# Routing of two expert mixtures in a twelve-block network on one core: choice by maxima, inversion on four column groups

## The chip, the cores and the metric

The kernel runs on one core of one Trainium2 chip. The metric is device time in microseconds (us) for one execution. Before the change the median of three runs is 3125.39 us (3124.48 to 3126.11).

The engines are named as the profile names them: PE is TensorE (matmuls), PEld its weight loads, DVE is VectorE, ACT is ScalarE, POOL is GpSimd, SP is SyncE, which only issues DMAs. Each engine works through its own list of instructions in order. A DMA issued by POOL or ACT stands in that engine's list like any other instruction.

## The reference

The network takes a latent array `x` of 16 sequences of 64 tokens with 256 channels (1024 tokens) and a context of 16 sequences of 1024 rows with 192 channels. Twelve blocks are applied one after the other, each as `x = x + block(layernorm(x))`: four times cross attention, a mixer (two Mamba kinds, a convolution, a second attention) and a feed-forward mixture of eight experts. The change touches the second and the last mixture. Cut to what they compute:

```python
# L1_ffn: every token goes to its two best experts
probs = softmax(xt @ gate_w.T)
top_w, top_i = top_k(probs, 2)
top_w = top_w / (top_w.sum(-1, keepdims=True) + 1e-9)
h = gelu(einsum('td,ndh->tnh', xt, w1) + b1)            # 256 -> 1024
out_all = einsum('tnh,nhd->tnd', h, w2) + b2            # 1024 -> 256
out = (take(out_all, top_i) * top_w[:, :, None]).sum(1)

# L3_ffn: the same with relu and no 1e-9, and each expert takes at most 256 choices;
# all first choices are counted before all second choices, in order of tokens
pos = place of the choice among those of its expert
valid = pos < 256
gate = topv * valid
out = sum over both choices of gate * (relu(xt @ w1[e] + b1[e]) @ w2[e] + b2[e])
```

`top_k` takes the lower index first where two values are equal. All is float32.

## The kernel before

The 1024 tokens lie as eight tiles of 128 partitions, `X[128, 8, 256]`. Each block normalizes `X` into `xn` (`layernorm`, L208) and transposes that into `xnT` (`norm_T`, L244), channels on partitions. A block's weights come through the pool `w` of five buffers, filled by DMAs on POOL's list (L169), which therefore also loads the weights of later blocks.

**The two mixtures** (`ffn1` L2438, `ffn3` L2553) don't compute all experts for all tokens. They sort the 2048 choices (J = 16 columns of 128: eight tiles for the first choice, eight for the second) into slots, gather the rows of `xn` for 128 slots at a time by an indirect DMA from a copy in DRAM, run them through one expert, scale them, and scatter them by an indirect DMA into a DRAM array `d_y` with one row for a choice. At the end `add_sent` (L2371) adds both rows of each token to `X`. ffn1 has 23 groups of 128 slots; a group belongs to one expert, found at run time, and its weights are gathered too (`up`, `down`, 1 MB each, three buffers). ffn3 has 16 groups, two for each expert, with weights loaded by plain DMAs.

What stands ahead of the loop over groups is done once in a block:

- `gate_logits` (L2151): 16 matmuls into `pgate`, copied to `s`. `softmax8` (L2159) with the exponential on ACT.
- `ranks` (L2178): each of the eight values of a token is compared with all eight, ties by index, so that the number of better ones is its rank `r`. These are passes over 8 x 64 elements.
- `choices` (L2245): `oh` marks expert and choice; a scan and two accumulating matmuls (`pq`) count, for each choice, those before it at the same expert.
- In ffn1 one more matmul (`pn`) gives the totals, from which `base` (where an expert's groups begin) and `whose` (which weight rows a group needs) follow.
- `slots` (L2268): for each choice its slot `sl`, the group as the one-hot row `at`, the lane in the group as the one-hot `inb[128, 16, 128]`. Multiplied by token number and by gate weight, `at` gives `val`. The inversion is 16 accumulating matmuls with `inb[:, j]` as the loaded weights and `val[:, j]` (46 or 32 columns) as the moving operand, into `pi`: for each lane and group the token and the weight. A few small DVE steps make `src` (row to gather), `to` (row to scatter) and `weight`.
- `add_down_bias` (L2190): transposes of the combine weights (`pc`), one copy (`combT`, nine rows with a row of ones), eight matmuls with nine rows each against the biases `downb` (`pb`), and eight additions to `X`.
- `take` (L2320) and `expert` (L2332): token gather, transposes (`pxg`), copy (`xT`), then for each of eight 128-wide hidden pieces the `pu` matmuls and an activation, then the `pd` matmuls and the scaling.

**What sets the order.** A scheduler at compile time places each instruction on its engine's list as soon as its inputs are ready in its own estimate, earlier program text first. Where `set_order(True)` is in force, instructions issued through `self.mm`, `self.tr` or a `Queue` (L183) are chained in the order of the program text for that engine (`in_order`, L172). Before the change neither mixture uses it. PSUM is shared out by `moe_pools` (L2234): two tiles of two banks (`big`) and four of one bank (`mid`).

Of the kernel before, what the change touches and what calls it, by code (L numbers as in the profile page):

```python
# [15 lines left out]
P = 128  # L16
# [62 lines left out]
class Net:  # L79
    def __init__(self, ctx, tc, a):  # L80
# [17 lines left out]
        self.downb = self.const.tile([9, 3, D], F32, name="downb")  # L98
        nc.scalar.dma_start(out=self.downb, in_=a["downb"])
# [12 lines left out]
    def make_masks(self):  # L112
# [27 lines left out]
        nc.gpsimd.iota(self.token, [[P, 2 * NT]], base=1, channel_multiplier=1, allow_small_or_imprecise_dtypes=True)  # L140

# [2048 lines left out]
    def add_down_bias(self, comb, i, big, mid, pool, more=None):  # L2190
# [8 lines left out]
        for t in range(NT):  # L2199
            tok = slice(t * P, (t + 1) * P)  # L2200
            ps = mid.tile([P, 512], F32, tag="m", name="pb")
            self.mm(ps[:, :D], cT[:, tok], self.downb[:, i, :], True, more is None)
            if more is not None:
                more(ps[:, :D], tok)
            nc.vector.tensor_tensor(self.X[:, t, :], self.X[:, t, :], ps[:, :D], ALU.add)
# [39 lines left out]
    def choices(self, r, one, mid):  # L2245
# [4 lines left out]
        oh = one.tile([P, 8, J], F32, name="oh")  # L2250
        upto = one.tile([P, 8, J], F32, name="upto")
        prev = one.tile([P, 8, J], F32, name="prev")
        on = one.tile([P, 8, J], F32, name="on")
        nc.gpsimd.memset(on, 1.0)
        nc.gpsimd.memset(on[:, :, 0], 0.0)
        for k in range(2):
            nc.vector.tensor_scalar(
                oh[:, :, k * NT : (k + 1) * NT], r.rearrange("p t e -> p e t"), float(k), None, ALU.is_equal
            )
        flat = [t.rearrange("p e j -> p (e j)") for t in (upto, on, oh)]  # L2260
        nc.vector.tensor_tensor_scan(flat[0], flat[1], flat[2], 0.0, ALU.mult, ALU.add)
        nc.vector.tensor_tensor(prev, upto, oh, ALU.subtract)
# [3 lines left out]
        return oh, pq[:, :P].rearrange("p (e j) -> p e j", e=8), upto  # L2266

    def slots(self, place, oh, s, one, mid, NG, keep):  # L2268
# [7 lines left out]
        sl, gate, low, t1, t2 = (one.tile([P, J], F32, name=f"sl{i}") for i in range(5))  # L2276
        tmp = one.tile([P, 8, J], F32, name="tmp")
        by_j = tmp.rearrange("p e j -> p j e")
        lane = one.tile([P, P], F32, name="lane")
        nc.gpsimd.iota(lane, [[1, P]], base=0, channel_multiplier=0, allow_small_or_imprecise_dtypes=True)  # L2280
        nc.vector.tensor_tensor(tmp, place, oh, ALU.mult)
        nc.vector.tensor_reduce(sl, by_j, AX.X, ALU.add)
        if keep:
            nc.vector.tensor_reduce(t1, oh.rearrange("p e j -> p j e"), AX.X, ALU.add)
            nc.vector.tensor_scalar(t1, t1, 1.0, -65536.0, ALU.subtract, ALU.mult)
            nc.vector.tensor_tensor(sl, sl, t1, ALU.add)

        at = one.tile([P, J, NG + 1], F32, name="at")
        inb = one.tile([P, J, P], F32, name="inb")
        val = one.tile([P, J, 2, NG], F32, name="val")  # L2290
        nc.vector.tensor_tensor(at, bc(sl, 2, NG + 1), bc(self.nth[:, : NG + 1], 1, J), ALU.is_ge)
        nc.vector.tensor_reduce(low, at[:, :, 1:], AX.X, ALU.add)
        nc.vector.scalar_tensor_tensor(low, low, -float(P), sl, ALU.mult, ALU.add)
        for h in range(4):
            js = slice(h * J // 4, (h + 1) * J // 4)
            nc.vector.tensor_tensor(inb[:, js], bc(low[:, js], 2, P), bc(lane, 1, J // 4), ALU.is_equal)
        nc.vector.tensor_tensor(at[:, :, :NG], at[:, :, :NG], at[:, :, 1:], ALU.subtract)
        nc.vector.tensor_tensor(val[:, :, 0], at[:, :, :NG], bc(self.token, 2, NG), ALU.mult)
        prod = one.tile([P, 8, J], F32, name="prod")
        for k in range(2):  # L2300
            ks = slice(k * NT, (k + 1) * NT)
            nc.vector.tensor_tensor(prod[:, :, ks], oh[:, :, ks], s.rearrange("p t e -> p e t"), ALU.mult)
        nc.vector.tensor_reduce(gate, prod.rearrange("p e j -> p j e"), AX.X, ALU.add)
        nc.vector.tensor_tensor(val[:, :, 1], at[:, :, :NG], bc(gate, 2, NG), ALU.mult)
        pi = mid.tile([P, 512], F32, tag="m", name="pi")
        for j in range(J):
            self.mm(pi[:, : 2 * NG], inb[:, j], val[:, j], j == 0, j == J - 1)

        row, weight, none, second = (one.tile([P, NG], F32, name=f"row{i}") for i in range(4))
        src, to = (one.tile([P, NG], I32, name=f"at{i}") for i in range(2))  # L2310
        nc.vector.tensor_scalar(row, pi[:, :NG], -1.0, None, ALU.add)
        nc.vector.tensor_scalar(second, row, float(N), -float(N), ALU.is_ge, ALU.mult)
        nc.vector.tensor_tensor(second, second, row, ALU.add)
        nc.vector.tensor_scalar(src, second, 0.0, None, ALU.max)
        nc.vector.tensor_copy(weight, pi[:, NG : 2 * NG])
        nc.vector.tensor_scalar(none, row, 0.0, 65536.0, ALU.is_lt, ALU.mult)
        nc.vector.tensor_tensor(to, row, none, ALU.add)
        return src, to, weight

    def take(self, src, g, n, d_x, pool):  # L2320

        xg = pool.tile([P, n, D], F32, tag="xg", name="xg", bufs=3)
        for i in range(n):
            self.nc.gpsimd.indirect_dma_start(
# [113 lines left out]
    def ffn1(self):  # L2438
# [6 lines left out]
        with ExitStack() as es:  # L2445
            one, two, big, mid = self.moe_pools(es, L)
            d_x, d_y = self.rows_dram(es, L)
# [281 lines left out]
```

## Time and profile before

| what | value |
|---|---|
| median of the runs | 3125.39 us |
| the profiled execution's own time | 3139.76 us |
| its span, first to last instruction | 3138.1 us |
| PE busy | 2942.0 us (94%) |
| DVE busy | 1966.8 us (63%) |
| ACT busy | 1340.0 us (43%) |
| POOL busy | 712.7 us (23%) |
| mean granted PE clock | 0.952 |
| ffn1: last gate matmul ends, first `pu` matmul starts | 1393.5, 1426.52 us |
| ffn1: loop over groups | to about 1612 us |
| ffn3: last gate matmul ends, first `pu` matmul starts | 2968.8, 3001.80 us |

How to read it: times inside the profile are counted from the start of the span of one profiled execution, which took 14 us longer than the median of the unprofiled runs. Lines L188 and L191 are the helpers `mm` and `tr`, and L72 is the helper `Queue`, so that operations are told apart by their tiles. In the lists of instructions a row has its start, its length, engine, line, operation, `output<-inputs`, shapes, a count, and in brackets the idle time of the engine before it with what ended that. A float32 matmul appears as two records. The granted clock of PE is 1.00 at full speed and 0.50 at half. The chain of waits is followed back from the last instruction, each step to what released it.

### The profile page before, as it was taken

The numbers are of one execution on the slowest core, as the hardware profiler recorded it, in microseconds if no ns is written. First come the engines' busy times: TensorE is split into PE (matmuls) and PEld (weight loads), VectorE is DVE, ScalarE is ACT, GpSimd is POOL, SyncE is SP. The second block draws the span as 40 slices with busy tenths as digits, with TensorE's granted clock in tenths as the row PEclk, the third lists the DMA queues.
The fourth block names the chain that finished last, engine by engine and source line by source line (L and its number), as shares of the span: only waits on it lengthen the run. The fifth ranks groups of instructions, "written<-read, shape, count | busy, mean of one in ns | idle before, by whom it ended". The sixth has DMA issues, their size and how long they took to land.

```text
span 3138.1 us, 64791 instructions
## 1 busy us (share of the span) xinstructions
PE 2942.0 (94%) x27232; PEld 1792.9 (57%) x27232; DVE 1966.8 (63%) x4085; ACT 1340.0 (43%) x3013; POOL 712.7 (23%) x780
## 2 busy tenths in 40 slices
PE   8999999898999999979978999997999899998797
PEld 4666666565555554458854555544655454546676
DVE  6888886523766656961127777768874667775511
ACT  3555554412554441003325444449851255554211
POOL 1000002400210001014410100026761454541131
PEclk9999999999999999968989999998999999999789
DMA  2001000014223313017751222201111111110233
GB/s 75 32 32 32 22 29 12 18 34 109 63 79 93 99 45 82 21 55 270 296 180 52 72 72 77 65 13 44 41 57 34 60 67 55 70 44 15 95 111 120
DMA packets 73796, 223.05 MB, mean 71 GB/s; under 512 B 17457, under 2 KB 28580, under 8 KB 66594
## 3 DMA queue, kind: packets, MB, share of 16 engines
q1 hardware_dynamic: 45936, 113.99, 11.9%
q0 software_dynamic: 21840, 99.39, 9.4%
q10 hardware_dynamic: 5730, 5.53, 0.6%
q8 instruction: 215, 3.52, 0.5%
q14 instruction: 75, 0.61, 0.1%
HBM read 210.00 MB, written 12.66 MB: 71 GB/s over the span
## 4 chain that ended last, share of the span: by engine, by line
PE 81%; DVE 7%; issue 5%; POOL 2%; ACT 2%; DMA 2%; SPq 0%; POOLq 0%; ACTq 0%; DVEq 0%
PE pss L188 15%; PE o L188 13%; PE psp L188 5%; PE pu L188 5%; PE pkv L188 5%; PE pd L188 5%; PE py L188 4%; PE pst L191 4%; PE psc L188 3%; PE po L188 2%; PE pb L191 2%; PE psq L188 2%; PE psi L188 1%; PE psy L188 1%; PE pg L188 1%
## 5 line engine op out<-in xcount | busy, mean ns | idle before, releaser
L188 PE MATMUL pss<-cT,qw 128*32 128x256 f32 x8192 | 367.7, 385 | 18.8 <-ACT pr L72 18.6
L72 DVE TENSOR_REDUCE nm<-pss 128x2 f32<-128x512 f32 (+1 forms) x384 | 309.5, 862 | 83.9 <-PE pss L188 83.9
L188 PE MATMUL o<-pT,cx 128*64 128x512 f32 (+3 forms) x1088 | 351.7, 576 | 0.0
L72 ACT ACTIVATE pr<-pss,nmm 128x256 f32<-128x256 f32 x512 | 234.8, 485 | 162.2 <-DVE nmm L72 162.2
L188 PEld LDWEIGHTS pss<-cT,qw 128*32 128x32 f32 x8192 | 203.2, 109 | 148.6 <-ACT pr L72 26.3
L188 PEld LDWEIGHTS o<-pT,cx 128*64 128x64 f32 (+1 forms) x1088 | 134.2, 163 | 188.4 <-issue 161.8
L205 POOL TENSOR_SCALAR rs<-mv 128x8 f32<-128x8 f32 (+3 forms) x50 | 9.7, 195 | 1006.3 <-DVE mv L221 534.0
L72 ACT ACTIVATE pr<-pr,sm 128x256 f32<-128x256 f32 x256 | 109.1, 497 | 203.1 <-DVE sm L72 203.1
L188 PE MATMUL pkv<-wx,cT 128*128 128x512 f32 (+1 forms) x512 | 193.3, 631 | 0.6 <-issue 0.6
L72 DVE TENSOR_SCALAR pr<-pr,sm 128x256 f32<-128x256 f32 (+1 forms) x384 | 170.1, 485 | 6.6
L72 DVE TENSOR_TENSOR_SCAN h<-dA,pb 128x512 f32<-128x512 f32 x128 | 154.7, 1217 | 16.0 <-PE pb L191 9.6
L1495 POOL TENSOR_TENSOR h<-h,cb 128x1024 f32<-128x1024 f32 x64 | 151.5, 2369 | 53.6 <-DVE h L72 51.2
L2355 DVE TENSOR_SCALAR y<-pd,row 128x256 f32<-128x256 f32 x39 | 18.9, 484 | 223.2 <-PE pd L188 192.7
L72 DVE STREAM_TRANSPOSE pT<-pr 128x1024 f32<-128x1024 f32 x128 | 151.8, 1224 | 2.2
L188 PE MATMUL pd<-wd,hT 128*128 128x256 f32 x656 | 149.3, 382 | 2.9 <-DVE hT L2543 1.4
L72 ACT ACTIVATE pr<-pss,nm 128x1024 f32<-128x1024 f32 x128 | 142.7, 1115 | 11.3 <-DVE nm L72 8.7
L191 PE MATMUL pst<-ident,pr 128*128 128x128 f32 x1024 | 141.5, 281 | 5.8 <-DVE sm L72 1.9
L191 PEld LDWEIGHTS pst<-ident,pr 128*128 128x128 f32 x1024 | 110.1, 141 | 62.1 <-ACT pT L72 26.5
L72 ACT COPY pT<-pst 128x512 f32<-128x512 f32 x128 | 75.0, 586 | 164.2 <-PE pst L191 164.2
L188 PEld LDWEIGHTS pd<-wd,hT 128*128 128x128 f32 x656 | 123.1, 190 | 31.4 <-DVE hT L2543 6.2
L188 PEld LDWEIGHTS pkv<-wx,cT 128*128 128x128 f32 (+1 forms) x512 | 64.5, 189 | 118.4 <-issue 92.2
L1669 POOL TENSOR_TENSOR rnk<-rnk,mhalf 128x8 f32<-128x8 f32 (+1 forms) x84 | 130.1, 1549 | 7.0
(525 smaller groups left out, 5795.5 us busy)
## 6 DMA issues: line engine op xcount, KB each, us to landing
cT<-in_ctxT SPq DMA_DIRECT2D x32, 768.0 KB, 4.3
cx<-in_ctxP SPq DMA_DIRECT2D x32, 768.0 KB, 4.2
cT<-in_ctxT SPq DMA_DIRECT2D x32, 512.0 KB, 4.1
cT<-in_ctxT SPq DMA_DIRECT2D x64, 256.0 KB, 5.3
offb<-d_off SPq DMA_DIRECT2D x16, 576.0 KB, 3.7
cb<-d_C SPq DMA_DIRECT2D x16, 512.0 KB, 4.1
wu<-in_L_ffn_w POOLq DMA_DIRECT2D x8, 1024.0 KB
wd<-in_L_ffn_w POOLq DMA_DIRECT2D x8, 1024.0 KB
```

Source lines behind the costliest of these rows:

```text
L72: ins = getattr(self.engine, op)(*args, **kwargs)
L188: self.in_order(self.nc.tensor.matmul(out, lhsT=lhsT, rhs=rhs, start=start, stop=stop))
L191: self.in_order(self.nc.tensor.transpose(out, in_, self.ident))
L205: nc.gpsimd.tensor_scalar(t[:p, :n], in_, scale, eps, ALU.mult, ALU.add)
L1495: nc.gpsimd.tensor_tensor(hs[i], hs[i], cbs[hf, g], ALU.mult)
L1669: nc.gpsimd.tensor_tensor(r, r, self.mhalf[:, : n * H], ALU.pow)
L2355: nc.vector.tensor_scalar(y[:, i, :], po[:, i * D : (i + 1) * D], weight[:, g + i : g + i + 1], None, ALU.mult)
```

## The change

For both mixtures it does the following.

- **Choice** (`choose`, in place of the copy of the logits, `softmax8`, `ranks` and `choices`): the best of eight by a maximum taken straight from PSUM, ties broken with a falling row 8, 7, ..., 1; the first choice is then pushed down by 4 in the exponentials and the second taken by another maximum. The probabilities are not divided by their sum; `over_both` divides by the sum of both chosen ones. A one-element Exp is issued ahead of it.
- **Order**: from the choice to the end of `slots` the instructions of PE, DVE, POOL and ACT issued through the helpers are chained in the order of the text.
- **Values on GpSimd**: the difference that makes `at` one-hot, the three products `val` and the combine weights `comb` are computed on POOL. In ffn1 the weight gathers of group 0 are chained on POOL ahead of `slots`.
- **Inversion to rows**: `val[:, k, j]`, padded to 32 columns, is now the loaded operand and `inb[:, j]` the moving one; choice j works on column group j mod 4, so each group of columns sums a quarter. The sums over the four are made by a matmul with `fold`, which also turns rows back to columns. Source tokens come first, so that the gather of the first rows is issued at once; weights and target rows follow (`pw`).
- **Biases**: `downb` is held four times, at partitions 0, 32, 64 and 96; the transposed combine weights `pc` are made on four column groups, the eight bias matmuls run on four row groups, and `X` gets two wide additions in place of eight.

The diff, cut to its core:

```diff
-        self.downb = self.const.tile([9, 3, D], F32, name="downb")
-        nc.scalar.dma_start(out=self.downb, in_=a["downb"])
+        self.downb = self.const.tile([P, 3, D], F32, name="downb")
+        for q in range(4):
+            nc.scalar.dma_start(out=self.downb[32 * q : 32 * q + 9], in_=a["downb"])
...
+        self.spot = const.tile([P, 2, NT], F32, name="spot")
+        for k in range(2):
+            nc.gpsimd.iota(
+                self.spot[:, k], [[P, NT]], base=0, channel_multiplier=1, allow_small_or_imprecise_dtypes=True
+            )
+        self.lane = const.tile([P, P], F32, name="lane")
+        nc.gpsimd.iota(self.lane, [[1, P]], base=1, channel_multiplier=0, allow_small_or_imprecise_dtypes=True)
+        self.falling = const.tile([P, 8], F32, name="falling")
+        nc.vector.tensor_scalar(self.falling, self.lane[:, :8], -1.0, 9.0, ALU.mult, ALU.add)
+        self.fold = const.tile([P, 32], F32, name="fold")
+        nc.vector.tensor_tensor(self.fold, self.ident[:, :32], self.ident[:, 32:64], ALU.add)
+        for q in (2, 3):
+            nc.vector.tensor_tensor(self.fold, self.fold, self.ident[:, 32 * q : 32 * q + 32], ALU.add)
...
-    def choices(self, r, one, mid):
+    def choose(self, wg, d_x, one, mid):
...
+        nc.scalar.activation(best[:, 3, 0:1], self.xn[:, 0, 0:1], AF.Exp)
...
+        self.set_order(True)
+        falling = bc(self.falling, 1, NT)
+        pg3 = pg[:, : NT * 8].rearrange("p (t e) -> p t e", e=8)
+        by_t = oh.rearrange("p e (k t) -> p k t e", k=2)
+        dve.tensor_reduce(best[:, 0], pg3, AX.X, ALU.max)
+        dve.tensor_tensor(d, pg3, bc(best[:, 0], 2, 8), ALU.subtract)
+        nc.scalar.activation(p, d, AF.Exp)
+        dve.scalar_tensor_tensor(w, d, 0.0, falling, ALU.is_ge, ALU.mult)
+        dve.tensor_reduce(best[:, 1], w, AX.X, ALU.max)
+        dve.tensor_tensor(by_t[:, 0], w, bc(best[:, 1], 2, 8), ALU.is_equal)
+        dve.scalar_tensor_tensor(d, by_t[:, 0], -4.0, p, ALU.mult, ALU.add)
+        dve.tensor_reduce(best[:, 2], d, AX.X, ALU.max)
+        dve.tensor_tensor(w, d, bc(best[:, 2], 2, 8), ALU.is_equal)
+        dve.tensor_tensor(w, w, falling, ALU.mult)
+        dve.tensor_reduce(best[:, 1], w, AX.X, ALU.max)
+        dve.tensor_tensor(by_t[:, 1], w, bc(best[:, 1], 2, 8), ALU.is_equal)
         flat = [t.rearrange("p e j -> p (e j)") for t in (upto, on, oh)]
+        dve.tensor_tensor_scan(flat[0], flat[1], flat[2], 0.0, ALU.mult, ALU.add)
+        dve.tensor_tensor(prev, upto, oh, ALU.subtract)
         pq = mid.tile([P, 512], F32, tag="m", name="pq")
         self.mm(pq[:, :P], self.leq, flat[2], True, False)
         self.mm(pq[:, :P], self.ones, prev, False, True)
+        dve.tensor_tensor(prod, by_t, bc(p, 1, 2), ALU.mult)
+        dve.tensor_reduce(gate, prod, AX.X, ALU.add)
...
+    def over_both(self, p, gate, eps, one):
+        dve = self.queue("dve", self.nc.vector)
+        z = one.tile([P, 2, NT], F32, name="z")
+        dve.tensor_tensor(z[:, 0], gate[:, 0], gate[:, 1], ALU.add)
+        if eps:
+            dve.tensor_reduce(z[:, 1], p, AX.X, ALU.add)
+            dve.scalar_tensor_tensor(z[:, 0], z[:, 1], eps, z[:, 0], ALU.mult, ALU.add)
+        dve.reciprocal(z[:, 0], z[:, 0])
+        return z[:, 0]
...
     (slots)
+        dve.tensor_tensor(tmp, place, oh, ALU.mult)
+        dve.tensor_reduce(sl, tmp.rearrange("p e j -> p j e"), AX.X, ALU.add)
+        dve.tensor_tensor(at, bc(sl, 2, NG + 1), bc(self.nth[:, : NG + 1], 1, J), ALU.is_gt)
+        dve.tensor_reduce(low, at[:, :, 1:], AX.X, ALU.add)
+        dve.scalar_tensor_tensor(low, low, -float(P), sl, ALU.mult, ALU.add)
+        pool.tensor_tensor(at[:, :, :NG], at[:, :, :NG], at[:, :, 1:], ALU.subtract)
+        spot = self.spot.rearrange("p k t -> p (k t)")
+        pool.tensor_tensor(val[:, 0, :, :NG], at[:, :, :NG], bc(spot, 2, NG), ALU.mult)
+        pc = mid.tile([P, 2, P], F32, tag="m", name="pc")
+        for k in range(2):
+            for q in range(4):
+                self.mm(pc[32 * q : 32 * q + 32, k, :], comb[:, 4 * k + q, :], self.ident)
+        cT = one.tile([P, 2, P], F32, name="cT")
+        act.copy(cT, pc)
+
+        def inverted(ps, k):
+            for j in range(J):
+                q = j % 4
+                self.mm(ps[32 * q : 32 * q + 32, :], val[:, k, j, :], inb[:, j], j < 4, j >= J - 4)
+
         for h in range(4):
             js = slice(h * J // 4, (h + 1) * J // 4)
+            dve.tensor_tensor(inb[:, js], bc(low[:, js], 2, P), bc(self.lane, 1, J // 4), ALU.is_equal)
+        pi = mid.tile([P, 512], F32, tag="m", name="pi")
+        inverted(pi[:, :P], 0)
+        rows = one.tile([P, 3, P], F32, name="rows")
+        dve.tensor_copy(rows[:, 0], pi[:, :P])
+        pf = mid.tile([P, 512], F32, tag="m", name="pf")
+        self.mm(pf[:, :32], rows[:, 0], self.fold)
+        src, to = (one.tile([P, NG], I32, name=f"at{k}") for k in range(2))
+        dve.tensor_copy(src, pf[:, :NG])
+        got = taken(src)
+        pool.tensor_tensor(gate, gate, bc(r, 1, 2), ALU.mult)
+        pool.tensor_tensor(val[:, 1, :, :NG], at[:, :, :NG], bc(gate.rearrange("p k t -> p (k t)"), 2, NG), ALU.mult)
+        pool.tensor_tensor(val[:, 2, :, :NG], at[:, :, :NG], bc(self.token, 2, NG), ALU.mult)
+        pb = [big.tile([P, 2, 2, D], F32, tag="b", name="pb") for _ in range(2)]
         for k in range(2):
+            for q in range(4):
+                rg = slice(32 * q, 32 * q + 9)
+                self.mm(pb[q // 2][:, q % 2, k, :], cT[rg, k, :], self.downb[rg, i, :])
+        pw = mid.tile([P, 2, P], F32, tag="m", name="pw")
+        for k in range(2):
+            inverted(pw[:, k, :], 1 + k)
+        act.copy(rows[:, 1:], pw)
+        for k in range(2):
+            self.mm(pf[:, 32 + 32 * k : 64 + 32 * k], rows[:, 1 + k], self.fold)
+        for h in range(2):
+            X = self.X.rearrange("p (k q) d -> p q k d", k=2)[:, 2 * h : 2 * h + 2]
+            dve.tensor_tensor(X, X, pb[h], ALU.add)
...
     (ffn1)
+            dve.tensor_tensor(place, pq, bc(base, 2, 2 * NT), ALU.add)
+            r = self.over_both(p, gate, 1e-9, one)
+            pool.tensor_tensor(comb[:, :, :8], prod[:, 0], prod[:, 1], ALU.add)
+            pool.tensor_tensor(comb[:, :, :8], comb[:, :, :8], bc(r, 2, 8), ALU.mult)
...
+            first = weights(0)
+            xg, src, to, weight = self.slots(
+                place, oh, r, gate, comb, val, 1, NG, one, big, mid, lambda src: self.take(src, 0, 1, d_x, two)
+            )
...
     (ffn3)
+            dve.scalar_tensor_tensor(oh, pq, float(CAP), oh, ALU.is_le, ALU.mult)
+            dve.tensor_tensor(place, pq, bc(base, 2, 2 * NT), ALU.add)
+            kept = one.tile([P, NT, 8], F32, name="kept")
+            by_t = oh.rearrange("p e (k t) -> p k t e", k=2)
+            pool.tensor_tensor(kept, by_t[:, 0], by_t[:, 1], ALU.add)
+            pool.tensor_tensor(kept, kept, p, ALU.mult)
+            pool.tensor_tensor(comb[:, :, :8], kept, bc(r, 2, 8), ALU.mult)
```

## The prediction

> **What bounds the kernel now.** I read the stretch table first, then the chain of waits, then the order of instructions inside the two stretches that the change rewrites. "Front" is what lies between the last gate matmul and the first `pu` matmul of expert 0: 1393.5 to 1426.52 us in ffn1, 2968.8 to 3001.80 us in ffn3, 33.0 us each.
>
> ```profile
> 1393.50:1400.60 7.10, 0.01 (x1) 0.00 (x0) 5.09 (x15) 1.54 (x2) 0.78 (x1) 0.50 0.41 148
> 1400.60:1411.20 10.60, 3.38 (x14) 2.23 (x14) 10.20 (x34) 0.00 (x0) 3.56 (x3) 0.50 0.20 69
> 1411.20:1418.30 7.10, 7.09 (x33) 7.00 (x33) 0.00 (x0) 1.28 (x1) 0.33 (x1) 0.50 0.85 343
> 1418.30:1425.40 7.10, 7.10 (x17) 5.06 (x18) 3.77 (x14) 0.00 (x0) 4.76 (x5) 0.50 0.38 108
> 1440.00:1600.00 160.00, 159.99 (x1013) 141.52 (x1013) 18.22 (x41) 59.56 (x162) 75.47 (x78) 1.00 0.79 291
> ```
>
> Columns: stretch, length, busy time of PE, PEld, DVE, ACT, POOL, granted clock, DMA share, GB/s. The front is serial: VectorE alone, then TensorE alone at half clock (0.50). From 1440 us the expert loop keeps TensorE busy all the time at clock 1.00, with DMA at 0.79. So a front that ends x us earlier moves the loop, and the end, by x us. ffn3's loop is the same case (PE busy 53.64 of 54.20 us from 3005.8 us, DMA share 0.47). The chain shows the TensorE part:
>
> ```profile
> 1411.21 7.06 PE pi L188 x32
> 1418.27 7.12 PE pb L188 x16
> 1425.39 0.63 PE pxg L2339 x2
> ...
> 2982.68 7.04 PE pi L188 x32
> 2989.71 1.72 PE pc L2195 x8
> 2991.46 1.22 DVE combT L2198
> 2992.81 7.16 PE pb L188 x16
> ```
>
> The x counts are records, two to a matmul in float32. The inversion `pi` has 16 matmuls, the biases `pb` eight.
>
> **Choice.** In ffn1 `choices` is reached 6.99 us after the logits (1393.55 to 1400.54), in ffn3 5.65 us (2968.81 to 2974.46). The difference is a table load, and five passes over 512 elements that follow each other at some 0.70 us:
>
> ```profile
> 1394.36 1.28 ACT L2165 ACT_TABLE_LOAD   x1 [3.84 <-DVE s L2164]
> 1396.69 0.69 DVE L2184 TENSOR_TENSOR gt<-s 128x512 f32<-128x512 f32 x1
> 1407.04 1.10 POOL L2488 DMA_INDIRECT up<-in_L_ffn_up,whose  x1 [12.45 <-DVE whose L2480]
> 1411.21 7.06 PE L188 MATMUL pi<-val,inb 128*128 128x46 f32 x32 [7.04 <-DVE val L2304]
> 1419.40 0.95 POOL L2324 DMA_INDIRECT xg<-L_ffnx,at  x1 [7.88 <-DVE at L2314]
> ```
>
> `choose` has eleven dependent VectorE steps over 64 elements or fewer; such steps start 0.26 us apart (copy 1393.55, maximum 1393.81, subtract 1394.07). 11 × 0.26 = 2.86 us, so `oh` is done at 1396.4 (saved 4.1) and 2971.7 (saved 2.8). ScalarE's exponential lies beside steps 3 to 5. The dummy Exp needs only `xn` of tile 0, and ScalarE is idle for 21.95 us before 1387.26, so the load costs nothing; without that cover, 1.3 us of ffn1 come back.
>
> **Placement, ffn1.** Scan and `prev` take 0.75 us, then `pq`'s second matmul 0.8. `pn` now stands behind it in TensorE's written order (it ran before it): `over` starts 2.05 us after `oh`, against 1.29. `over` to `base` 1.6 (as now), `end` to `whose` 1.3, `place` 0.3, `over_both` with eps 0.9: VectorE is at 1402.55. Then `tmp`, sum, `at`, two for `low`: 2.0; four `inb` comparisons 2.45 (as at 1407.8): done at 1407.0. GpSimd runs beside it in written order: second `comb` step 0.3 after `r`, `up` and `down` gathers of group 0 with their gaps 2.9, so it is free at 1405.75, when `at` is there already. Its two steps over 368 elements then end the stage. I cost them from these GpSimd rows of 256 and 512 elements:
>
> ```profile
> L1093 POOL TENSOR_TENSOR tapp<-tapl,tapi 128x256 f32<-128x256 f32 x16 | 9.9, 621 | 20.1 <-DVE tapl L72 10.7 <-DVE taps L72 9.4
> L924 POOL TENSOR_TENSOR vd<-after,dtA 128x512 f32<-128x512 f32 x8 | 8.1, 1042 | 13.5 <-DVE dtA L72 8.5 <-PE pe L188 5.0
> ```
>
> Between them, 0.9 us each (0.85 to 1.4: the 512-element rows at L1016 spread from 1.05 to 1.57). Inversion starts at 1407.6, against 1411.21: the stage itself is half a microsecond longer, because the values wait for the two gathers on GpSimd's queue. A third gather put between them would cost 1.25 more.
>
> **Inversion and biases on groups.** Eight 32x512 matmul records on four row groups take 1.07 us on the chain, against 8 × 0.43 = 3.4 (a 256-column record at full clock is 0.215): a factor 3.2. For column groups:
>
> ```profile
> 47.35 0.94 PEld L188 LDWEIGHTS o<-pT,v 128*32 128x32 f32 x64 [0.81 <-issue]
> 47.35 1.10 PE L188 MATMUL o<-pT,v 128*32 128x64 f32 x64
> ```
>
> 64 records at 64 columns in 1.10 us, 17 ns each. At half clock a record of 128 columns costs 0.22 (`pi`), so 32 of them 2.2 us at factor 3.2, not 7.06; `pb` 7.12/3.2 = 2.2. Bounds: 1.75 (factor 4) and 7.06 (none). The Trainium skill, "TensorE: Matmul & The Clock Gate", Part 3, speaks against this: a weight load overlaps running matmuls only where row groups differ, and column groups share all rows; "LDWEIGHTS" gives columns/1.2 ns, 27 ns a load. By it each inversion costs 32 × 27 = 0.85 us more, three to a site, 5.1 us in all. In the row above loads and matmuls together take 17 ns, less than such a load alone; I go by the row.
>
> From 1407.6: inversion 2.2, copy of `rows` 0.35, fold 0.4, `src` 0.2: 1410.75. Token gather from 1411.0 (0.95). It moved its data 1.6 to 2.35 us after its start before (1419.40, DMA 1421.00 to 1421.75), so it is there at 1413.6. Behind it on GpSimd: `gate` 0.3, two value steps 0.9 each, to 1414.15. TensorE meanwhile: `pb` to 1412.6, then `pw` 2 × 2.2 from 1413.2 to 1417.6, ScalarE's copy 0.45, folds 0.5, `pxg` 0.7, `xT` 0.5: 1419.7, or 1418.7 if the transposes slip into the copy's gap. I take 1419.2 against 1426.52: **7.3 us**. The two wide `X` additions (1.2 us each, by the 128x1024 rows) lie under `pw`. The loop's weights: 2 MB of group 0 at the 400 GB/s seen at 1411 to 1415 end near 1410.5; later groups need 2 MB per 7.8 us against 5.2 at that rate, so the loop doesn't wait.
>
> **ffn3.** After `oh` at 2971.7: 0.75, then `pq` to 2973.25 with `prod` and `gate` (0.7) beside it, `over_both` 0.4, `oh` and `place` 0.6, five steps 1.75, `inb` 2.45: 2978.35. No gather precedes GpSimd's values (0.7 each at 256 elements), they end at 2976.7. The inversion runs behind `inb` and ends at 2978.9, against 2989.72: 10.8 saved. Then 0.95 to `src`, two token gathers to 2982.3, `gate` and values to 2984.05, `pw` to 2987.75, copy and folds 0.95, `pxg` 1.1, `xT` 0.75: 2990.55, or 2990.1 in the gap. Taken 2990.3 against 3001.80: **11.5 us**. `combT`'s copy (1.22) and the separate `pc` wait are in that.
>
> **The rest.** Three more `downb` issues (0.6 us each) push `X`'s second half on ScalarE's queue, needed only near 49.8 us; three more iotas (0.15 to 0.24) fit GpSimd's 0.87 us wait before 8.12. Bounds 0 to 0.6, taken 0.2. The new memsets replace `combT`'s 0.94 and `lane`'s 0.24.
>
> Sum: 7.3 + 11.5 − 0.2 = 18.6 us. Profiled span 3138.1 becomes 3119.5. The runs' median lies 12.7 us below that span; the same 18.6 gives **3106.8 us**.
>
> The clock is the second place where page and trace differ. Part 1 of the same page says that some 3.4 us of sustained work lift the clock from half to full. Here the clock stays 0.50 through `pi`, `pb` and on to 1432, 20 us of nearly unbroken work. By the page `pw`'s second half, folds and transposes would run twice as fast, 1.7 us a site: 22 us in all. I take 18.6.
>
> **Rivals.** A measurement of this kernel can tell about 0.2%, 6 us, from no change.
> - *GpSimd sets the pace.* If value steps run at 1.4 and a gather slips ahead of them, ffn1 loses 1 + 1.25 before the inversion and 1 after, ffn3 1.2; a clock that rises 3 us later costs 1.5 a loop, 3 in all. Together 7.5, gain 11: 3114. For: GpSimd is empty in the fronts only because it did nothing there. Against: ffn3's values have 1.6 us of slack.
> - *The fronts shrink more*: the clock rises, factor 4, `pxg` and `pu` ahead of `pw`. Gain 23 to 31: 3098.
> - *The groups don't overlap*, so the change doesn't do what it says. `pi` 7.06, `pb` 7.16, `pw` 14.1 in a row: first `pu` at 1438.7 and 3009, 12.2 + 7.2 later: 3145, slower. It decides below a factor of 1.5 (56.6/f us of group work against 37 us of room). The two rows above speak against it.
> - *Nothing reaches the end*, because the loops wait for weights instead: 3125. Against: DMA share 0.79 and 0.47.
>
> **Numbers.** Main case (gain 14 to 23) 0.62; GpSimd 0.17 (7 to 14); more 0.13; slower 0.05; same 0.03. The first three are faster: 0.92. The range 3097 to 3117 leaves out the last two and the far ends of the second and third; the main case alone is 3102 to 3111.
>
> **What would show it.** `oh` 2.9 us after the logits and no table load between; `pi` near 2.2 us; first `pu` 25 to 26 us after the logits in ffn1, 21 to 22 in ffn3; clock 0.50 throughout; loops of the same length. `pi` over 4 us, or idle TensorE inside the loops, would prove me wrong.

## The result and the profile after

Over 20 executions each, the kernel before takes 3135.27 us (3124.48 to 3144.13) and the changed one 3124.04 us (3103.28 to 3131.57). The ratio is 0.9963, 95% interval 0.995 to 0.9976: 11.6 us faster, between 7.5 and 15.7. The forecast was 3106.8 us and a gain of 18.6. The direction held; the time lies 17.2 us above the forecast and outside its range.

These 17.2 us have two parts. The three executions that I started from (median 3125.39) lay at the low edge of what the kernel before does; 20 of them have a median 9.9 us higher. The other 7.4 us are gain that did not come (18.6 − 11.2, the difference of the medians).

The profile tells where. Each figure is counted from the end of the last gate matmul; "last `pu`" is the start of the last `pu` matmul of the loop, so it also shows what the loop gives back.

| | before | predicted | after | after, second profile |
|---|---|---|---|---|
| ffn1, first `pu` | 33.0 | 25.7 | 29.0 | 29.3 |
| ffn1, last `pu` | 217.5 | 210.2 | 214.8 | 213.8 |
| ffn3, first `pu` | 33.0 | 21.5 | 23.5 | 22.2 |
| ffn3, last `pu` | 144.6 | 133.1 | 133.1 | 131.7 |

At the end of ffn3 the predicted 11.5 us are there. At the end of ffn1 only 2.7 to 3.7 of the 7.3 are. By these rows the change is worth 14.2 us in the first profile and 16.6 in the second.

The stretch table of the changed kernel, ffn1 and then ffn3 (columns: stretch, length, busy PE, PEld, DVE, ACT, POOL, clock, DMA share, GB/s):

```profile
1395.14:1398.20 3.06, 0.00 (x1) 0.00 (x0) 2.57 (x11) 0.26 (x1) 0.78 (x1) 0.50 0.33 76
1398.20:1410.90 12.70, 2.68 (x22) 2.03 (x23) 9.84 (x28) 0.37 (x1) 6.11 (x7) 0.50 0.48 175
1410.90:1418.60 7.70, 4.66 (x54) 3.17 (x58) 2.21 (x4) 0.00 (x0) 5.01 (x7) 0.50 0.95 379
1418.60:1424.20 5.60, 4.78 (x71) 4.12 (x71) 1.04 (x2) 1.47 (x2) 2.83 (x4) 0.50 1.00 394
...
2982.29:2988.46 6.17, 5.70 (x72) 4.14 (x72) 0.69 (x1) 0.37 (x1) 3.90 (x5) 0.60 0.39 85
2988.46:3000.00 11.54, 11.40 (x56) 9.54 (x56) 1.47 (x6) 3.78 (x8) 2.51 (x4) 1.00 0.29 84
```

The choice takes 3.06 us, as predicted (2.86). What is new in ffn1 stands at the end of the third and fourth row: the DMA share is 0.95 and 1.00. Before, it was 0.85 and 0.38 in the last two stretches of the front. In ffn3 the experts start at clock 1.00 (last row). The chain of waits names the step, here through ffn1's front:

```profile
1404.87 1.12 POOL up L72
1405.99 0.30 issue
1406.29 1.50 POOL down L72
1407.78 0.84 POOL at L72
...
1408.78 1.23 POOL up L72
1410.02 0.83 POOL val L72
1410.90 2.91 PE pi L205 x32
...
1415.30 7.57 DMA xg<-L_ffnx,at
...
1423.00 0.66 PE pxg L2438 x2
```

Two things differ from the prediction. At 1408.78 GpSimd issues the `up` gather of group 1 ahead of the first value step. And group 0's token rows, 128 KB, need 7.57 us from their issue to their landing, against the 2.6 that I took. `pxg` waits for them to 1423.00. The rows end last, but not by much here: `pw` ends at 1422.18, 27.0 us after the logits, where I had 24.1. In ffn3 the chain has no transfer, but a late value:

```profile
2973.86 2.46 PE pi L205 x32
...
2979.23 0.96 POOL xg L72
...
2980.60 0.10 POOL xg L72
2980.70 0.90 issue
2981.61 0.64 POOL val L72
...
2982.29 5.21 PE pw L205 x64
```

The token gather for the second expert (2980.60, 1.0 us) sits between `gate` and the value that `pw` waits for.

### The profile page after: what moved, and what is told of

Its sections match the earlier page's. It is cut to its first block, busy times and chain, and to the rows that moved or that the text cites. A ratio compares the mean times of both kernels' runs of the same rounds, so it can differ in the third digit from the quotient of the medians.

```text
span 3122.8 us, 65112 instructions
## 1 busy us (share of the span) xinstructions
PE 2929.8 (94%) x27388; PEld 1779.5 (57%) x27388; DVE 1957.9 (63%) x4053; ACT 1340.7 (43%) x3019; POOL 719.5 (23%) x800
## 4 chain that ended last, share of the span: by engine, by line
PE 82%; DVE 7%; issue 4%; POOL 3%; ACT 2%; DMA 2%; SPq 0%; POOLq 0%; DVEq 0%; ACTq 0%
PE pss L205 15%; PE o L205 13%; PE pu L205 6%; PE psp L205 6%; PE pkv L205 5%; PE pd L205 5%; PE py L205 4%; PE pst L208 4%; PE psc L205 3%; PE po L205 2%; PE pb L208 2%; PE psq L205 2%; PE psi L205 1%; PE psy L205 1%; PE pg L205 1%
## 5 line engine op out<-in xcount | busy, mean ns | idle before, releaser
L72 ACT ACTIVATE pr<-pss,nm 128x1024 f32<-128x1024 f32 x128 | 142.5, 1114 | 11.2 <-DVE nm L72 8.6
```

The source lines that it names most:

```text
L72: ins = getattr(self.engine, op)(*args, **kwargs)
```

## The experiments

Theories. T1: the missing time is the order on GpSimd's queue. The text chains what stands in `slots`, but gathers of later groups come from the loop and may go in anywhere between. T2: TensorE's groups are slower than costed. T3: the totals only show how long TensorE was granted half clock. All fronts and ends:

| run | median us (n) | ratio to before, 95% | ffn1 first / last `pu` | ffn3 first / last `pu` |
|---|---|---|---|---|
| changed, again | 3120.61 (11) | 0.9948 (0.9923 to 0.9974) | 29.3 / 213.8 | 22.2 / 131.7 |
| later gathers held back | 3113.42 (10) | 0.9932 (0.9912 to 0.9952) | 24.0 / 208.3 | 21.7 / 133.2 |
| values on VectorE | 3103.28 (5) | 0.9908 (0.9875 to 0.9941) | 22.3 / 208.3 | 19.7 / 129.3 |
| the same, weights of group 1 first | 3115.61 (10) | 0.9929 (0.9903 to 0.9956) | 26.4 / 210.7 | 19.7 / 129.3 |
| changed, old choice | 3113.26 (6) | 0.9948 (0.9923 to 0.9972) | 31.9 / 215.1 | 25.0 / 134.6 |
| changed, one column group | 3130.31 (12) | 0.9988 (0.9969 to 1.0008) | 35.0 / 217.1 | 31.1 / 140.7 |
| changed, dense fill | 3124.78 (10) | 0.9955 (0.9931 to 0.998) | 29.6 / 213.2 | 22.7 / 132.2 |
| VectorE and dense fill | 3111.26 (5) | 0.9911 (0.9875 to 0.9946) | 21.8 / 208.3 | 19.4 / 128.9 |
| VectorE, shorter ffn1 | 3132.21 (12) | 0.9977 (0.9958 to 0.9996) | 27.1 / 220.2 | 23.0 / 134.6 |
| VectorE again | 3123.01 (12) | 0.9953 (0.9932 to 0.9973) | 27.8 / 212.6 | 23.0 / 135.4 |
| VectorE, `pw` on one group | 3110.24 (4) | 0.9917 (0.989 to 0.9944) | 27.5 / 209.7 | 25.0 / 134.5 |
| VectorE, third time | 3114.60 (5) | 0.9936 (0.9916 to 0.9957) | 22.4 / 209.3 | 19.7 / 129.3 |

### The changed kernel once more

> The changed kernel once more, with nothing edited. In its first profile the first rows copy of ffn1 started 1.0 us after the modelled end of pi, and pxg waited in ffn1 for token rows that landed 7.6 us after their gather was issued. T1 (order on GpSimd's queue, which the compiler fixes): the fronts repeat, 29 us in ffn1 and 23.5 in ffn3, within 1 us. T3 (luck): one or both are off by 2 us or more, the one-microsecond tails are gone or elsewhere. The time: 3124 us, single executions from 3103 to 3132.

The fronts repeat: 29.3 and 22.2 us. The 1.0 us gap behind `pi` in ffn1 is gone (0.07), and so is the one behind ffn3's `pw`, which is most of the 1.3 us there. In ffn1 this gains nothing: `pw` ends 25.9 us after the logits instead of 27.0, and `pxg` starts at 28.4, because the token rows land at 28.3:

```profile
1398.32 9.04 DMA xg<-L_ffnx,at
```

So the landing ends last in both profiles; without it `pxg` would have come 0.8 us earlier in the first and some 2.5 us earlier in this one. T3 is wrong for the fronts.

It is right for the totals. The two profiles of the same code span 3122.8 and 3103.6 us, at a mean clock of 0.955 and 0.963. Of these 19.2 us, 16 arise in one place, the convolution block ahead of ffn1, which the change doesn't touch. The stretch table of both profiles:

```profile
1310.00:1375.00 65.00, 64.19 (x580) 40.71 (x579) 43.96 (x70) 8.74 (x15) 1.45 (x2) 0.58 0.07 19
```

```profile
1310.00:1375.00 65.00, 61.24 (x655) 42.95 (x654) 55.15 (x100) 10.82 (x18) 6.23 (x14) 0.87 0.12 33
```

Clock 0.58 against 0.87 in the same 65 us, and more work done in the second. Half-clock windows add to 281 and 234 us in all: 47 us more at half clock go with 19.2 us more time.

### Later gathers held back

```diff
+            self.hold(g, ins)   # up, down, xg of groups from 1 on
...
+    def hold(self, g, ins):
+        if g:
+            order = mybir.DependencyInfo(mybir.DependencyClass.NoSync, mybir.DependencyReason.DATA)
+            self.tc.add_manual_dep(ins.ins, self.behind, order, reason="behind the values")
```

`self.behind` is the last of the three value steps.

> Gathers of the later groups (up, down and xg from group 1 on) stay behind the last value step on GpSimd; nothing else changes. Measured from the last routing logit to the first up multiplication pu, which is 29.0 us in ffn1 and 23.5 us in ffn3 of the changed kernel. T1 (the lost time is GpSimd's queue: two gathers of 1.4 us in ffn1 and one in ffn3 slipped between the values): 26.2 in ffn1 and 22.1 in ffn3. T2 (the groups of TensorE are slower than costed, and the queue lies beside them): 28.5 to 29.5 and 23 to 24. Against this, the later gathers start about 3 us later: if they are late for their groups, ffn1's loop grows by what the front gained. The time then: T1 about 4 us under the changed kernel, T2 the same.

GpSimd's list in ffn1's front (start, length, idle time before):

```profile
1391.70 0.84 POOL L72 TENSOR_TENSOR at<-at 128x368 f32<-128x368 f32 x1
1392.62 1.15 POOL L72 TENSOR_TENSOR val<-at,spot 128x368 f32<-128x368 f32 x1
1397.30 0.99 POOL L72 DMA_INDIRECT xg<-L_ffnx,at  x1 [3.53 <-DVE at L72]
...
1399.38 0.81 POOL L72 TENSOR_TENSOR val<-at,token 128x368 f32<-128x368 f32 x1
1400.33 0.98 POOL L72 DMA_INDIRECT up<-in_L_ffn_up,whose  x1
```

ffn1's front falls from 29.0 to 24.0 us, more than T1 asked for (26.2), and the last `pu` goes with it (208.3 against 214.8): the later weights are not late for the loop. ffn3 falls to 21.7; its last `pu` doesn't, since there the clock came back only 3.9 us into the loop. T2 falls: TensorE's code is untouched. `src` comes 1.5 us earlier than in the second profile of the changed kernel (17.4 against 19.0), `pw` ends 2.8 us earlier (23.0 against 25.9), and the rows land 2.8 us after their issue instead of 9.0. So this edit removes both delays at once; the next experiments part them.

### Values on VectorE, and then the weights first

```diff
-        pool.tensor_tensor(val[:, 0, :, :NG], at[:, :, :NG], bc(spot, 2, NG), ALU.mult)
+        dve.tensor_tensor(val[:, 0, :, :NG], at[:, :, :NG], bc(spot, 2, NG), ALU.mult)
...
     (the subtraction in at, gate and both other values likewise)
```

> The subtraction in at, the gate's product and the three value tensors go to VectorE; GpSimd keeps the gathers and comb. T1: VectorE writes the four lane comparisons of inb at the 2.45 us that they took before (3.54 and 3.23 us beside GpSimd's steps), the values take about 0.35 us each and no gather can come between them; the front falls from 29.0 to 25 to 26 us in ffn1 and from 23.5 to 21.5 in ffn3, and the inversion of gate and token can begin before the copy of src. T2: pw still ends no sooner than 8 us after pi's copy, the front falls by less than 1 us. If instead VectorE becomes the bound (five more steps, some 2 us, in its order ahead of src), the front is the same or 1 us longer.

Fronts of 22.3 and 19.7 us, 6.7 and 3.8 below the first profile of the changed kernel, better than expected. `inb` is back at its old length; changed kernel and VectorE kernel:

```profile
1405.64 3.54 DVE L72 TENSOR_TENSOR inb<-sl,lane 128x512 f32<-128x512 f32 x4
```

```profile
1406.63 2.49 DVE L72 TENSOR_TENSOR inb<-sl,lane 128x512 f32<-128x512 f32 x4
```

In the first, three of the four steps take 0.69 us and the one beside GpSimd's subtraction 1.72. In ffn1 a value takes 0.54 us on VectorE, 0.82 to 1.15 on GpSimd.

In this kernel GpSimd has nothing but gathers. That allows the transfer to be tested alone:

```diff
-            first = weights(0)
+            first, second = weights(0), weights(1)
```

> The kernel with the values on VectorE, and in ffn1 the weight gathers of group 1 issued ahead of slots, so before group 0's token rows. GpSimd is free by then (four gathers, done 14 us after the logits; src is ready at 15.9), so this tells queue time apart from transfer time. If the token rows wait behind 4 MB of weights in the transfer engines: they land 24.5 to 25 us after the logits instead of 20.6, and ffn1's front is 26 to 26.5 us instead of 22.3. If only GpSimd's own time counts: landing and front as before, 20.6 and 22.3. ffn3 is untouched: 19.7.

The token gather is issued 16.16 us after the logits, as without the edit (16.14), and `pw` ends at 21.27 (21.24). But the rows land at 25.1, and the first `pu` is at 26.4 instead of 22.3. From the chain:

```profile
1407.54 8.93 DMA xg<-L_ffnx,at
1416.47 0.14 issue
1416.61 0.67 PE pxg L2438 x2
```

Both are what was written for the transfer engines. The landing without the edit is not recorded in the first VectorE profile; the third profile of the same kernel has it in its chain, at 1415.26, which is 20.0 us after the logits:

```profile
1411.37 3.89 DMA xg<-L_ffnx,at
```

So 2 MB of weights that are asked for ahead of the token rows delay them by some 5 us, although GpSimd issues the rows at the same moment. The other profiles agree. In the second profile of the changed kernel, in the one-column-group kernel and in the dense fill, the rows are issued 19.2, 21.9 and 17.9 us after the logits, and land at 28.3 in all three, 0.4 us behind the last of the five weight gathers ahead of them. When the rows are asked for hardly matters there; what is ahead of them does.

All these gathers go through one DMA queue (q0 in the trace, 5.31 of 5.34 MB between 1400 and 1417 us), so the runs don't tell whether the rows wait for their turn in that queue or for their share of the engines. The Trainium skill, "DMA: Bandwidth & Descriptors", section "Issuing engines are not separate DMA queues", says that all DMAs run on the same 16 engines and interleave there, whichever engine issued them. Whether rows asked for through another queue would land sooner, no run here tried.

### The old choice

```diff
-        dve.tensor_reduce(best[:, 0], pg3, AX.X, ALU.max)
...
+        dve.tensor_copy(p, pg3)
+        self.softmax8(p)
+        self.ranks(w, p, 8, one)
```

> Undoes one part alone: the choice by two maxima gives way to softmax and ranks, all else as changed. The prediction's costing of this part: oh comes 2.8 us later (5.7 instead of 2.9 us after the last logit), and the first pu is later by as much in both fronts: 31.8 and 26.3 us. If the choice is not on the path, the fronts stay at 29.0 and 23.5. T3 (the totals are the clock's luck): the time moves by anything up to 10 us whatever the front does.

`oh` is done 5.7 us after the logits instead of 3.0, and the first `pu` comes at 31.9 and 25.0: 2.6 and 2.9 us later than in the second profile of the changed kernel (2.9 and 1.5 later than in the first, where ffn3's `pw` had its late end). The choice is on the path in both fronts and its price was right. The total (3113 us) is below that of the kernel that it lengthens: differences of 3 us can't be read from totals here.

### One column group

```diff
-                q = j % 4
-                self.mm(ps[32 * q : 32 * q + 32, :], val[:, k, j, :], inb[:, j], j < 4, j >= J - 4)
+                self.mm(ps[:32, :], val[:, k, j, :], inb[:, j], j == 0, j == J - 1)
```

> Undoes one part alone: all 16 inversion multiplications write to one group of 32 columns, one accumulation chain, and the fold adds 32 rows; all else as changed. If four groups run beside one another (the prediction: a factor near 4), pi goes from 1.9 to 7 us, gate and token from 3.6 to 13 us or, with no wait for the values between, 14; the front grows by 5 us to src and by about 12 us to the first pu: 41 in ffn1 and 35 in ffn3, and the time by 23 us. T2 (they overlap by less): the growth is less than half of that. The clock may rise within the longer run of multiplications, which would take up to half of the growth back.

From the chain of ffn1:

```profile
1407.80 5.38 PE pi L205 x32
...
1417.67 8.85 PE pw L205 x64
```

`pi` takes 5.4 us where four groups take 1.9, `pw` 8.85 against 3.6. These are not yet the factors of the overlap, because the clock rises in the middle of the one-group `pi`:

```profile
1407.80:1411.26 3.46, 3.46 (x17) 2.88 (x18) 0.00 (x0) 0.00 (x0) 1.91 (x2) 0.50 0.88 344
1411.40:1413.20 1.80, 1.77 (x17) 1.50 (x14) 0.00 (x0) 0.00 (x0) 0.00 (x0) 1.00 0.94 397
```

At half clock (0.50, first row) its records start 213 ns apart, at full clock 109. The changed kernel's `pi`, all of it at half clock:

```profile
1410.90:1412.84 1.94, 1.94 (x32) 1.38 (x32) 0.00 (x0) 0.50 0.93 355
```

Here four records, one for each group, start within 20 ns, and the next four 213 ns after the first. So at equal clock the factor is 4.0: the groups overlap fully. Before the change, with 128 columns loaded and 46 moving, the records of `pi` started 213 ns apart too. The swap of operands by itself gains nothing at half clock; the fall from 7.06 us is the groups'.

The fronts grow by 5.9 and 7.6 us, half to two thirds of the 12 that I expected, and the ends by 2.3 and 7.6. By the front of ffn1 alone T2 would pass (less than half of 12); what shortens it is the rise of the clock, which the expectation allowed for, and not a weaker overlap. In ffn1 the clock is also at 1.00 before the first expert, and the loop then takes 182.2 us instead of 185.8.

### Dense fill against the half clock

```diff
+    def warm(self, n, mid):
+        ps = mid.tile([P, 512], F32, tag="m", name="pwarm")
+        for _ in range(n):
+            self.mm(ps, self.xn[:, 0, :P], self.xnT[:, 0, :512])
```

> The changed kernel with seven dense multiplications of 512 columns put into TensorE's idle time in each front of ffn1 (one before the choice, four behind pn, one behind pc, one behind pb; ffn3 has no four behind pn); their results are not used. They take 1.7 us each at half clock. Clock theory (the granted clock follows how densely TensorE streams, and the fronts run at 0.50 because it is idle or loads weights): the clock is at 1.00 in part of ffn1's front, its first 32 pu records are 2 us quicker, and the front is as long as before or 1 us shorter: time 3 to 5 us under the changed kernel. Rival (the clock needs unbroken work, so fill of this kind does nothing): it stays 0.50 through the front and the fill only delays comb's and the values' multiplications, front 0 to 2 us longer.

Stretches of ffn1's front:

```profile
1379.19:1389.20 10.01, 6.72 (x14) 3.56 (x14) 8.45 (x34) 0.26 (x1) 1.66 (x4) 0.50 0.31 106
1389.20:1396.00 6.80, 3.79 (x54) 1.74 (x52) 4.33 (x7) 0.37 (x1) 5.86 (x7) 1.00 0.74 258
1396.00:1402.80 6.80, 6.80 (x64) 4.27 (x68) 2.53 (x3) 0.00 (x0) 5.83 (x8) 0.50 0.98 402
```

The fill lifts the clock for 6.8 us, and it is lost again in the next stretch although PE counts as busy all of it. The front is as long as before (29.6), because the token rows land at 28.3 in this kernel too. The first 32 `pu` records are 0.9 us quicker, not 2, and the time shows no gain. A faster TensorE buys nothing while the transfer ends last.

> Values on VectorE and the dense fill together. If both gains are independent: fronts 22.3 less 0 to 1 and 19.7 less 0 to 1, first pu at full clock in both, time 2 to 4 us under that of the values on VectorE alone. If the fill does nothing to the clock: fronts 0 to 2 us longer, no gain.

Without that transfer it buys 0.5 and 0.3 us, at the low end of what was expected. The time, 3111 us, is not below the VectorE kernel's; the two gains are too small to tell there.

### A shorter ffn1, and VectorE again

```diff
+            self.mm(pn[:, :8], self.ones, upto[:, :, J - 1])
         self.mm(pq[:, :P], self.ones, prev, False, True)
...
+        if i == 1:
+            biases()      # pb ahead of pi
```

> Values on VectorE, and three more steps of ffn1 in another order: the totals pn ahead of the second multiplication of pq (0.75 us earlier), the biases pb ahead of pi, where TensorE is idle, and every gather of a later group behind group 0's token gather. From the rows of the kernel with the values on VectorE: whose and src come 0.75 us earlier, the token rows land at 19.8 us, pw ends at 19.4 instead of 21.25; ffn1's front 21.2 us instead of 22.3, ffn3's 19.7 as there. If the token rows still land 4.4 us after their issue, they are what is left of the bound. The time: that of the values on VectorE less 1 us, which no timing here can tell from nothing.

> The kernel with the values on VectorE once more, unedited, beside the former. Fronts 22.3 and 19.7 us within half a microsecond, since nothing on its path waits for a late transfer. Time: by the fronts alone (6.7 to 7.0 and 2.5 to 3.8 us shorter than the changed kernel's in its two profiles), 3111 to 3114; the five executions at 3103 were luck of the clock if it is this, and something beyond the fronts gained if the median stays under 3106.

Neither expectation held. The unedited VectorE kernel has fronts of 27.8 and 23.0 us here, against 22.3 and 19.7. These two runs shared a chip that no other experiment here used. `pw` in ffn3, VectorE again and then the third time, where all is as in the first:

```profile
L205 PE MATMUL pw<-inb,val x64: 269/421/423, 2965.8 to 2971.6; 128*32 128x128 f32 x64
L72 ACT COPY rows<-pw x1: 372/372/372, 2973.3 to 2973.3; 128x256 f32<-128x256 f32 x1
```

```profile
L205 PE MATMUL pw<-inb,val x64: 421/421/423, 2972.4 to 2975.7; 128*32 128x128 f32 x64
L72 ACT COPY rows<-pw x1: 372/372/372, 2976.1 to 2976.1; 128x256 f32<-128x256 f32 x1
```

The same 64 records start over 5.8 us instead of 3.3, with gaps of up to 1.3 us, and the copy behind them begins 1.7 us after the last start instead of 0.5. In the shorter ffn1 the copy waits 6.4 us. The edit did what it should up to there (`src` 0.5 us earlier, `pw`'s last start at 19.4). Its loop is also longer than that of the VectorE kernel on the same chip, 193.2 against 184.9 us; why is open. So it is no improvement as it stands.

> Values on VectorE, with the gate and token inversion pw alone on one column group instead of four; pi stays on four. In the last two profiles pw on four groups took 6 us and more in ffn3 (14.2 to 20.3 us after the logits, with gaps of 0.7 and 1.3 us between its records) where three earlier profiles of the same code show 3.6. If dense streaming on four groups brings the stall on: none here, pw lasts the 9 to 10 us that the one-column-group kernel showed, front 28 to 29 us in ffn1 and 25 to 26 in ffn3, whatever the next run shows. If the stall comes from elsewhere, it shows here too.

> The kernel with the values on VectorE a third time, as the control. If the stall belongs to the kernel: pw again 6 us, fronts 27.7 and 22.9. If it belongs to the chip or the moment: pw 3.6 us, fronts 22.3 and 19.7 as in the first profile, and then the former run tells nothing of its cause.

The control shows no stall (22.4 and 19.7), so the kernel on one group says nothing about it. What stalls `pw` stays open: it is in all four fronts on one chip and in none of the eight fronts of the VectorE kernels with this `pw` on others. The late end of ffn3's `pw` in the first profile of the changed kernel looks like a smaller one: gaps of 0.2 and 0.3 us among its last records, and a copy 1.1 us late. The kernel on one group shows another thing. Its ffn1 front is 5.1 us longer than the control's, yet its last `pu` is only 0.4 us later. In the control, group 1's rows arrive late, after the first experts began; its table of waits from 1417 to 1440 us has the line

```profile
PE pxg L2438 <- DMA xg<-L_ffnx,at: 3.4, 1, 3.4
```

The weights of groups 1 and 2 land 27.0 and 32.9 us after the logits there, the row behind each group's weights later still. A part of the difference is the clock, which falls back to half for 3.4 us in the control's first experts and not in those of the other. A cleaner sign is in the table: with later gathers held back, with the values on VectorE, and with the fill added to that, the first `pu` comes at 24.0, 22.3 and 21.8 us, and the last at 208.3 in all three (209.3 in the third VectorE profile, from 22.4). So in these kernels an ffn1 front below 24 us buys nothing at the end, and the prediction's "a front that ends x us earlier moves the loop, and the end, by x us" stops holding there.

## Why the prediction was wrong, point by point

- **The base.** "The same 18.6 gives 3106.8" rests on three executions at 3124 to 3126. In 20, eight lie at 3124 to 3128 and twelve at 3134 to 3144. This step alone is 9.9 of the 17.2 us. The page of the profiled execution said 3139.76, and I treated that as the odd one.
- **ffn1's token rows: the step of the mechanism that failed.** "It moved its data 1.6 to 2.35 us after its start before (...), so it is there at 1413.6." That row was read with nothing else in transfer: before the change three 1 MB weight gathers had been issued, and in the 1.15 us ahead of the token gather nothing moved (the last two columns, DMA share and GB/s, are zero):

```profile
1418.25:1419.40 1.15, 1.15 (x4) 0.96 (x4) 0.82 (x7) 0.00 (x0) 0.00 (x0) 0.50 0.00 0
```

In the changed kernel five are issued ahead (up to the `up` gather of group 2). In its second profile the fifth lands 27.9 us after the logits and the token rows at 28.3; in the first profile the rows land at 27.7. Before, their data had moved by 1421.75, 28.2 us after the logits. So the rows for which the whole front was shortened came half a microsecond earlier, or not at all. 2 MB more ahead of them cost some 5 us where a run changed nothing else.
- **ffn1's values: the same gathers a second time.** I had `pw` end 24.1 us after the logits; it ended at 27.0 and 25.9. The inversion started at 15.8 instead of 14.1, mostly because one `up` gather slipped ahead of the first value (1.23 us), and a token gather slipped ahead of the other two; the late copy behind `pi` adds 1.0 us in the first profile. With the rows in time the front would still have been some 28.2 and 26.8 us (an estimate: the waits of `pxg`, 0.8 and 2.5 us, taken off), not 25.7. Holding the later gathers back cures both and gives 24.0. ffn1's term measured 2.7 to 3.7 us at the end of the loop instead of 7.3.
- **ffn3.** 11.5 predicted, 11.5 and 12.8 measured at the last `pu`, but of other parts: the front is 9.5 and 10.9 shorter (one gather slipped, and `inb` took 3.2 us instead of 2.45), and some 2 us come from experts that start at clock 1.00 (their first 32 `pu` records take 7.2 us instead of 9.1). "Clock 0.50 throughout" was wrong there.
- **Right.** The choice (3.0 us measured, 2.9 predicted), no table load ahead of `oh`, `pi` 1.9 us and `pb` 2.1 us (2.2 each predicted), `pw` 3.6 us (4.4 predicted), and loops of nearly the same length. The column groups overlap by a factor of 4.0 instead of 3.2, which the rule of the Trainium skill on weight loads ("TensorE: Matmul & The Clock Gate", Part 3) made doubtful; by the prediction's estimate from it `pi` would take some 3.0, against the 1.9 measured. The price of a record with 128 moving columns was right by luck: its 0.22 was read from the old `pi`, which loads 128 columns and moves 46; the one-group kernel shows 0.213 for 128.
- **The gain as timed.** 11.6 us (7.5 to 15.7) and, in the second timing, 16.3 (8.2 to 24). The profiles' 14.2 and 16.6 lie in the second interval, and 14.2 in the first. What is left between 11.6 and 14.2 is within the spread of single executions.

The rival that came true is GpSimd's, in one half: a gather slipped ahead of the values, as it said, but the value steps were not slow (0.82 us, against the 1.4 it feared). It left out the larger cost, that such a gather also puts 1 MB ahead of the token rows. That its gain of 11 is close to the measured 11.6 is therefore luck in part.

**A better version.** With the values on VectorE the kernel is faster than before in all three timings (ratios 0.9908, 0.9953 and 0.9936, each interval below 1). Against the changed kernel two of its three profiles have ffn1's last `pu` 4.5 to 6.5 us earlier and ffn3's 2.5 to 3.8; in totals the first VectorE timing lies below the first one of the changed kernel, the other intervals overlap, so the gain is clear in the profile only. In the profile with the stall ffn3's end is later than the changed kernel's by 2.3 to 3.7 us. In ffn1 holding back the later gathers gives the same end (208.3).

## What to carry to other kernels

When a change moves a small gather behind a point where an engine becomes free, list every transfer that may be issued ahead of it, in bytes: here they set its latency. An order written out for a part of the program fixes that part alone; what a later loop issues on the same queue can be put between its steps. And where single executions spread by 20 us, take the base from as many of them as the result will be taken from, and judge parts by the profile's own stages.

## What the runs showed that I had not expected

- **GpSimd and VectorE slow each other.** A comparison of 512 elements on VectorE with two inputs in SBUF took 1.72 us beside a GpSimd subtraction of 0.84, and 0.69 alone. The Trainium skill, "GPSIMD Engine Reference", section "Key points", says that the two engines contend when VectorE reads two inputs from SBUF. The trace agrees, and shows that VectorE lost 1.03 us, more than the length of GpSimd's step. GpSimd loses too: in the kernel with later gathers held back its value step beside a comparison took 1.15 us, against 0.82 alone.
- **Half-clock windows come in steps of 3.4 us** (3.4, 6.8, 10.2, 13.7, 20.5 in the profiles), and dense fill of four 1.7 us multiplications did lift the clock, while 20 us of `pi` and `pb` before the change did not. That agrees with the 3.4 us of the Trainium skill ("TensorE: Matmul & The Clock Gate", Part 1) only if not all busy time counts. The one-column-group kernel says so too: its `pi`, with 128 columns moving to 32 loaded, brought the full clock 3.5 us after it began, while the old `pi`, at the same 213 ns a record with 46 moving to 128 loaded, did not in 7.06 us. Nor did the old `pb`, 256 columns moving but nine rows, in the 7.12 us after it. What counts is open; no run here varied one of these alone.
- **An accumulation group's end is late in some profiles.** `rows` started 1.0 us after `pi`'s modelled end in one profile of the changed kernel, 0.07 us in the next, and the copy came 1.4 to 6 us after `pw`'s modelled end on one chip.
